# Rows of two degree tables: one-hot products on TensorE in place of 98 gathers

## The chip, the cores and the metric

The kernel runs on one core of a Trainium2 chip. The metric is the device time of one execution in microseconds (us). Times are given as the median of several runs; the profile comes from one further execution.

## The reference

The model is a two-layer graph network on 6250 nodes with 256 features and 100,000 edges. Each layer adds a graph part, a mixing part and a feed-forward part with experts to `x`. The change concerns the graph part of the second layer:

```python
in_deg = jnp.minimum(segment_sum(ones, dst, num_nodes), MAX_IN_DEGREE - 1)    # MAX = 512
out_deg = jnp.minimum(segment_sum(ones, src, num_nodes), MAX_OUT_DEGREE - 1)
edge_proj = edge_attr @ W_sum + b_sum
sum3d = segment_sum(edge_proj, src, num_nodes)
cent_term = sigmoid(centralities @ W_cent + b_cent)
vor_term = sigmoid(voronoi_values @ W_vor + b_vor)
return x + z_in[in_deg] + z_out[out_deg] + cent_term + vor_term + sum3d
```

`z_in` and `z_out` are tables of 512 rows of 256 numbers. Every node takes one row of each, chosen by its in-degree and its out-degree.

## The kernel before

Nodes lie in 49 tiles of 128 (the last has 106), called NT; edges lie in 782 tiles of 128, called W1C. All numbers are f32.

**The stage around the change.** The function `middle` first chooses two experts for each node (`gating`), then runs, in this order, `experts`, `take_back` and `mix1`; the function `between` follows. `experts` runs 32 slots of 512 node rows, and each of the 4 steps of a slot has 2 halves: two 128x512 products (L1417) and a Gelu on ScalarE (L1419), and, for the slot before, four 128x256 products (L1425) and an addition on VectorE (L1427). Eight transposes (L1400) turn the next slot's rows. Weights (512 KB each), rows and biases come by SyncE's queue (SP), and so does the store of the results (L1433). `take_back` gathers two expert results for each node tile (98 gathers). `mix1` goes over the nodes twice, 13 groups of up to 4 tiles each, in 15 iterations.

**The work behind it.** Behind this foreground runs a chain of background work, written as Python generators: `edge_sums`, which is `edge_pass` (L620) over the 782 edge tiles, beside `others`: `gat_places` (49 row gathers) and then `node_terms`, the function of the change. For an edge tile, `edge_pass` gathers 128 rows by GpSimd (POOL; `gather`, L776), marks a one-hot matrix on VectorE (`mark`, L616), multiplies both on TensorE (L603) and, once every 4 tiles, adds the result on VectorE (L594). The rows go to a ring of 15 tiles, with the gather 11 tiles ahead of its product and the mark 8 ahead.

**What sets the order.** Each engine runs its instructions in the order in which the program writes them. That order is dealt out by hand: every generator yields the due cost of what it has just written, and the foreground calls `step(us)`, which advances the background until its due costs cover the call:

```python
def step(self, us):
    while self.behind is not None and us > self.ahead:
        cost = next(self.behind, None)
        ...
        self.ahead += cost
    self.ahead -= us

def beside(self, work, other, rate):
    due = 0.0
    for cost in work:
        yield cost
        due += rate * cost
        while other is not None and due > 0.0:
            cost = next(other, None)
            ...
```

`beside` lets `others` run with `edge_sums` at 0.7 units for each unit of edges; an edge tile yields 1.27 units. `experts` calls `step(3.8)` eight times a slot, `take_back` once `step(20.0)`, `mix1` 30 times `step(11.0)`. What is left of the background then is written out by `finish`.

**Node terms.** For each node tile, `node_terms` forms two tanh terms (L1519, L1520), gathers one row of each table for its 128 nodes (tiles `zg`, through L776), and for the tile before adds all up on VectorE (L1528 to L1533) and stores the sum to DRAM on SP (L1534, `terms`). `between` reads it later. It yields 30 + 2 units at first, then 1.0 + 2 x 1.27 a tile for making and 1.0 a tile for adding.

Other names: `BT` is a buffer of 128 x 12544 numbers in SBUF, of which `experts` uses the first 8192 columns; `mm()` takes the next of PSUM's banks of that name, 4 in this stage, used in turn; `node_column` writes a row of degrees to DRAM and turns it into a column for each node tile; `indeg` and `outdeg` are these columns.

Of the kernel before, what the change touches and what calls it, by code (L numbers as in the profile page):

```python
# [8 lines left out]
F32 = mybir.dt.float32  # L9
I32 = mybir.dt.int32  # L10
AF = mybir.ActivationFunctionType
OP = mybir.AluOpType
# [6 lines left out]
P = 128  # L19
N = 6250  # L20
NT = 49
NP = NT * P
LAST = N - (NT - 1) * P
C = 256
# [36 lines left out]
class Net:  # L61


    def __init__(self, ctx, tc, a, out):
        self.ctx, self.tc, self.nc, self.a, self.out = ctx, tc, tc.nc, a, out
        self.const = ctx.enter_context(tc.tile_pool(name="const", bufs=1))
        self.dram = ctx.enter_context(tc.tile_pool(name="dram", bufs=1, space=DRAM))
        self.scat = 0
        self.behind = None


# [623 lines left out]
    def node_column(self, row, name, dst):  # L695

        nc = self.nc
        flat = self.dram.tile([NT, P], F32, name=f"flat_{name}")
        nc.sync.dma_start(flat.rearrange("(o t) p -> o (t p)", o=1), row)
        with self.tc.tile_pool(name="column", bufs=1, side="right") as sp:  # L700
            tiles = sp.tile([NT, P], F32, name="tiles")
            nc.sync.dma_start(tiles, flat)
            pt = self.tr()
            nc.tensor.transpose(pt[:, 0:NT], tiles, self.ident[0:NT, 0:NT])
            nc.vector.tensor_copy(dst, pt[:, 0:NT])
# [784 lines left out]
    def node_terms(self, pool):  # L1490


        nc, a = self.nc, self.a
        self.terms = self.dram.tile([NP, C], F32, name="terms")
        bsum = self.vec(pool, "L1_gnn_b_sum")
        base = self.vec(pool, "L1_mix_b_out")
        parts = []
        for w, b, v in (("L1_gnn_W_cent", "L1_gnn_b_cent", "node_vec1_n2"),
                        ("L1_gnn_W_vor", "L1_gnn_b_vor", "node_vec1")):
            c = pool.tile([P, NT], F32, name=f"nv_{v}")  # L1500
            nc.vector.memset(c, 0.0)  # L1501
            with nc.allow_non_contiguous_dma(reason="one value a node"):
                nc.sync.dma_start(c[:, 0:NT - 1], a[v][0:(NT - 1) * P, :].rearrange("(t p) o -> p (t o)", p=P))
                nc.sync.dma_start(c[0:LAST, NT - 1:NT], a[v][(NT - 1) * P:N, :])
            parts.append((self.vec(pool, w), self.vec(pool, b), c))
        yield 30.0

        nc.vector.tensor_scalar(base, base, 1.0, None, op0=OP.add)
        idx = pool.tile([P, 2, NT], I32, name="zidx")
        nc.vector.tensor_scalar(idx[:, 0, :], self.indeg, 511.0, None, op0=OP.min)  # L1510
        nc.vector.tensor_scalar(idx[:, 1, :], self.outdeg, 511.0, None, op0=OP.min)
        yield 2.0
        begun = None
        for t in list(range(NT)) + [None]:
            if t is not None:
                s = [pool.tile([P, C], F32, name=f"sg{i}", bufs=2) for i in range(2)]
                z = [pool.tile([P, C], F32, name=f"zg{i}", bufs=2) for i in range(2)]
                for i, (w, b, c) in enumerate(parts):
                    nc.vector.scalar_tensor_tensor(s[i], w, c[:, t:t + 1], b, op0=OP.mult, op1=OP.add)  # L1519
                    nc.scalar.activation(s[i], s[i], AF.Tanh, scale=0.5)  # L1520
                    yield 0.5
                for i, name in enumerate(("L1_gnn_z_in", "L1_gnn_z_out")):
                    self.gather(z[i], a[name], idx[:, i, t:t + 1])
                    yield 1.27
            if begun is not None:
                t0, s0, z0 = begun
                x = s0[0]
                nc.vector.tensor_add(x, x, s0[1])  # L1528
                nc.vector.scalar_tensor_tensor(x, x, 0.5, z0[0], op0=OP.mult, op1=OP.add)
                nc.vector.tensor_add(x, x, z0[1])  # L1530
                yield 0.5
                nc.vector.tensor_add(x, x, base)
                nc.vector.scalar_tensor_tensor(x, bsum, self.outdeg[:, t0:t0 + 1], x, op0=OP.mult, op1=OP.add)  # L1533
                nc.sync.dma_start(self.terms[t0 * P:(t0 + 1) * P, :], x)  # L1534
                yield 0.5
            begun = None if t is None else (t, s, z)

    def middle(self, scales, sums):
        nc = self.nc
        self.sumsT = sums.tile([P, 1, NP], F32, name="sumsT")  # L1540
        nc.vector.memset(self.sumsT, 0.0)
        self.mixed = sums.tile([P, 2, C], F32, name="mixed")
        self.norms1 = self.norms(sums, "mix1")
        self.chosen = self.dram.tile([8 * CAP, C], F32, name="chosen")
        self.yielded = self.dram.tile([TAKEN * SLOT, C], F32, name="yielded")
        self.rows_out = 0
        with self.tc.tile_pool(name="takes", bufs=1) as tp:
            self.shares = tp.tile([P, 2, NT], F32, name="shares")
            self.pos = tp.tile([P, 2, NT], I32, name="pos")
            self.slot = tp.tile([1, 2, TAKEN], I32, name="slot_of")  # L1550
            with self.tc.tile_pool(name="biases", bufs=1) as bp:
                self.expert_biases(bp)
                self.gating(scales)
            with self.tc.tile_pool(name="edge", bufs=1, reuse_waits="tile") as edge:
                def others():
                    yield from self.alone(self.gat_places)
                    yield from self.alone(self.node_terms)
                self.after_this(self.beside(self.edge_sums(edge), others(), 0.7))
                with self.tc.tile_pool(name="ffn0", bufs=1, reuse_waits="tile") as pool:
                    self.experts(pool, 3.8)  # L1560
                    self.take_back(pool)
                with self.tc.tile_pool(name="mix1", bufs=1, reuse_waits="tile") as mp:
                    self.mix1(mp)
                with self.tc.manual_schedule():
                    self.finish()
        self.edge_pass_if(self.wide2, self.sumsT, None, self.a["edge_attr_128"], self.by_src,
                          EDGE_BITS, E1 - 1, None)

    def mix1(self, pool):


        nc, tc, a, BT = self.nc, self.tc, self.a, self.BT
# [16 lines left out]
        def at(i):  # L1589
            return quads[i] if 0 <= i < nq else None  # L1590
        nc.scalar.activation(sd, mv[:, :, 1], AF.Sqrt, bias=self.eps)
        self.invert(norms, 0, NT)
        with tc.manual_schedule():
            for i in range(nq + 2):
                if at(i):
                    t, n, _ = at(i)
                    for q in range(n):
                        x = self.xa[:, t + q, :]
                        nc.vector.tensor_scalar(x, x, mv[:, t + q, 0:1], r[:, t + q:t + q + 1],
                                                op0=OP.subtract, op1=OP.mult)  # L1600
                if at(i - 1):
                    t, n, _ = at(i - 1)
                    for j, pt in enumerate(self.turned(lambda q: self.xa[:, t + q, :], n)):
                        nc.scalar.copy(BT[:, j, t * P:(t + n) * P], pt)
                if at(i - 2):
                    t, n, m = at(i - 2)
                    k = n * P if m == P else m
                    pk = self.mm()
                    self.dense(pk[:, 0:n * P], w[:, :, P:2 * P], BT[:, :, t * P:(t + n) * P])
                    nc.vector.tensor_reduce(tops[:, i - 2:i - 1], pk[:, 0:k], axis=AX.X, op=OP.max)  # L1610
                    nc.scalar.copy(kT[:, t * P:t * P + n * P], pk[:, 0:n * P])
                self.step(11.0)
            top = pool.tile([P, 1], F32, name="top")
            nc.vector.tensor_reduce(top, tops, axis=AX.X, op=OP.max, negate=True)
            cx = self.mm("kv")
# [1 line left out]
            for i in range(nq + 2):  # L1617
                if at(i):
                    t, n, m = at(i)
# [3 lines left out]
                if at(i - 1):  # L1623
                    t, n, m = at(i - 1)
# [5 lines left out]
                if at(i - 2):  # L1630
                    t, n, m = at(i - 2)
                    ek = eks.pop(i - 2)
                    for q in range(n):
                        nc.tensor.matmul(cx[:, 0:C], lhsT=ek[:m, q, :], rhs=self.xa[:m, t + q, :],
                                         start=(t + q == 0), stop=(t + q == NT - 1))
                self.step(11.0)
        total = pool.tile([P, 1], F32, name="total")
        nc.vector.tensor_reduce(total, parts, axis=AX.X, op=OP.add)
        nc.vector.reciprocal(total, total)
# [509 lines left out]
```

## Time and profile before

| | |
|---|---|
| median of 3 runs | 5470.35 us (5465.84 to 5480.0) |
| the profiled execution | 5465.94 us, span 5464.2 us |
| PE busy (TensorE matmul) | 3804.3 us, 70% of the span |
| POOL busy (GpSimd) | 3682.1 us, 67% |
| DVE busy (VectorE) | 2738.3 us, 50% |
| ACT busy (ScalarE) | 1239.7 us, 23% |
| gathers of edge attributes | 782, mean 959 ns |
| gathers of table rows (`zg`) | 98, first at 3012.0 us, last at 3453.1 us |
| take-back gathers | 98, first at 3577.1 us, last at 3710.6 us |
| mean granted clock of TensorE | 0.753 |

PE is TensorE's matmuls, PEld its weight loads, DVE VectorE, ACT ScalarE, POOL GpSimd, SP SyncE with its DMA queue. A group of instructions is named by line, engine, operation, written and read tiles and shape; behind it stand its busy time, the mean of one in ns, and the idle time of its engine just before, with what ended it. "Issue" is idle time in which the engine waited for nothing that the profile shows. The granted clock is the share of TensorE's full clock.

### The profile page before, as it was taken

What the parts mean: (1) busy time and instruction counts of PE and PEld (TensorE: products, weight loads), DVE (VectorE), ACT (ScalarE), POOL (GpSimd) and SP (SyncE); (2) the same over time, 40 slices, a digit from 0 to 9 for tenths busy, and PEclk for the clock granted to TensorE, in tenths of its full rate; (3) what the DMA queues carried; (4) which work ended last, traced back from release to release, by engine and by line L of the source; (5) the groups of instructions that cost most, each with busy time, mean ns of one, the idle gap of its engine ahead of it and who ended that gap; (6) DMA issues with size and microseconds to landing.
All of it is one profiled execution on the core that took longest, in us unless ns stands there. A gap on an engine that the chain in (4) does not pass through costs nothing. (4 is left out here: it accounts for less than half of the span.)

```text
span 5464.2 us, 56784 instructions
## 1 busy us (share of the span) xinstructions
PE 3804.3 (70%) x16292; PEld 2792.4 (51%) x16292; DVE 2738.3 (50%) x7767; ACT 1239.7 (23%) x2840; POOL 3682.1 (67%) x4400
## 2 busy tenths in 40 slices
PE   5898989997677777884476788705676975875400
PEld 4666666664556666654354555503555653543300
DVE  6886655535887666437453555345334212212217
ACT  4994333335000000015111222101002211111100
POOL 1767777770777777742574777777754888888861
PEclk8778576668896566675698999957667997987755
DMA  5334333331333333332377555432224222222234
GB/s 189 116 96 135 88 94 92 89 100 58 98 106 98 96 99 99 107 87 74 135 260 161 160 176 166 127 90 58 53 68 121 69 54 45 64 54 41 51 92 160
DMA packets 382785, 563.75 MB, mean 103 GB/s; under 512 B 124687, under 2 KB 270278, under 8 KB 382286
## 3 DMA queue, kind: packets, MB, share of 16 engines
q0 software_dynamic: 150864, 331.19, 22.4%
q1 hardware_dynamic: 207812, 209.55, 12.2%
q10 hardware_dynamic: 23756, 18.97, 1.1%
q8 instruction: 140, 2.29, 0.2%
q14 instruction: 213, 1.74, 0.1%
HBM read 446.11 MB, written 113.72 MB: 102 GB/s over the span
## 5 line engine op out<-in xcount | busy, mean ns | idle before, releaser
L603 PE MATMUL es<-hot,ring 128*128 128x128 f32 x7820 | 1897.9, 374 | 722.7 <-DVE sumsT L594 211.5
L776 POOL DMA_INDIRECT ring<-table,src_of x1564 | 1616.2, 1033 | 778.0 <-issue 226.8
L603 PEld LDWEIGHTS es<-hot,ring 128*128 128x128 f32 x7820 | 1436.2, 250 | 1131.4 <-issue 313.9
L776 POOL DMA_INDIRECT ring<-in_edge_attr,edge_of x782 | 749.7, 959 | 321.9 <-PE es L603 130.9
L776 POOL DMA_INDIRECT G<-gtab,glist x800 | 787.4, 984 | 189.9 <-issue 155.5
L2067 PE MATMUL mm<-lw,lhT 128*128 128x256 f32 x1568 | 380.4, 385 | 223.5 <-ACT lhT L2061 172.3
L640 ACT ACTIVATE ring<-ring,w_of 128x256 f32<-128x256 f32 x782 | 385.8, 507 | 519.6 <-DMA ring<-table,src_of 484.9
L2067 PEld LDWEIGHTS mm<-lw,lhT 128*128 128x128 f32 x1568 | 301.5, 193 | 350.1 <-ACT lhT L2061 175.8
L594 DVE TENSOR_TENSOR BT<-BT,es 128x256 f32 x392 | 163.9, 418 | 497.7 <-PE es L603 496.5
L2059 PE MATMUL mm<-lxt,lw 128*128 128x512 f32 (+1 forms) x832 | 380.7, 584 | 33.9 <-DVE ly L2069 31.5
L618 DVE TENSOR_SCALAR hot<-numbers,node_of,w_of 128x128 f32<-128x128 f32 x782 | 292.7, 401 | 59.5 <-PE es L603 58.8
L2069 DVE TENSOR_TENSOR ly<-mm,lb 128x256 f32<-128x256 f32 x196 | 81.1, 423 | 475.3 <-PE mm L2067 471.2
L1425 PE MATMUL mm<-mw,BT 128*128 128x256 f32 x1024 | 262.7, 403 | 39.6 <-DVE nv_node_vec_n L1501 22.0
L616 DVE TENSOR_SCALAR hot<-numbers,node_of 128x128 f32<-128x128 f32 x782 | 242.5, 337 | 64.2 <-PE es L603 63.6
L1417 PE MATMUL mm<-BT,mw 128*128 128x512 f32 x512 | 259.1, 631 | 6.1 <-ACT BT L1401 4.0
L616 DVE TENSOR_SCALAR hot<-numbers,from_of 128x128 f32<-128x128 f32 x782 | 241.7, 345 | 22.3 <-PE es L603 22.1
L2061 ACT ACTIVATE lhT<-mm,lb 128x512 f32<-128x512 f32 (+1 forms) x208 | 136.9, 664 | 465.6 <-PE mm L2059 465.2
L2059 PEld LDWEIGHTS mm<-lxt,lw 128*128 128x128 f32 x832 | 160.0, 198 | 143.7 <-issue 100.9
L1425 PEld LDWEIGHTS mm<-mw,BT 128*128 128x128 f32 x1024 | 197.1, 203 | 66.5 <-DVE nv_node_vec_n L1501 22.9
L1304 POOL DMA_INDIRECT chosen<-z,pos x98 | 99.0, 1011 | 178.4 <-DVE chosen L1227 133.6
L611 PE MATMUL es<-hot,ones 128*1 128x128 bf16 x782 | 189.2, 242 | 0.0
L1855 DVE TENSOR_TENSOR ge<-G,ad 128x320 f32<-128x320 f32 x10 | 9.5, 949 | 342.0 <-DMA G<-gtab,glist 341.9
(531 smaller groups left out, 4757.8 us busy)
## 6 DMA issues: line engine op xcount, KB each, us to landing
mw<-in_L_ffn_W SPq DMA_DIRECT2D x64, 512.0 KB
ring<-table,src_of POOLq DMA_INDIRECT x1564
ye<-ly SPq DMA_DIRECT2D x48, 512.0 KB
yes<-ye SPq DMA_DIRECT2D x48, 512.0 KB
xs<-chosen SPq DMA_DIRECT2D x32, 512.0 KB
yielded<-BT SPq DMA_DIRECT2D x32, 512.0 KB
G<-gtab,glist POOLq DMA_INDIRECT x800
ring<-in_edge_attr,edge_of POOLq DMA_INDIRECT x782
```

Source lines behind the costliest of these rows:

```text
L594: nc.vector.tensor_tensor(dst, dst, ps[:, 0:h * P].rearrange("p (j n) -> p j n", j=h), op=OP.add)
L603: nc.tensor.matmul(ps[:, j * P:(j + 1) * P], lhsT=rows[:, j * P:(j + 1) * P], rhs=hot, start=(first and j == 0), stop=(last and j == h - 1))
L611: self.nc.tensor.matmul(ps, lhsT=self.ones16[:, 0:1], rhs=half, start=False, stop=False)
L616: self.nc.vector.tensor_scalar(dst, self.numbers, node, None, op0=OP.is_equal)
L618: self.nc.vector.tensor_scalar(dst, self.numbers, node, w, op0=OP.is_equal, op1=OP.mult)
L640: nc.scalar.activation(r, r, AF.Copy, scale=w[:, i:i + 1])
L776: self.nc.gpsimd.indirect_dma_start(out=dst, out_offset=None, in_=table, in_offset=bass.IndirectOffsetOnAxis(ap=idx, axis=0))
L1417: nc.tensor.matmul(ph, lhsT=w1s[s][:, j, c * P:(c + 1) * P], rhs=xTs[s % 2][:, j, :], start=(j == 0), stop=(j == 1))
L1425: nc.tensor.matmul(po[:, :C], lhsT=hTs[(s - 1) % 2][:, i, c * P:(c + 1) * P], rhs=w[:, i, :], start=(i == 0), stop=(i == 3))
L2059: nc.tensor.matmul(ph[:, :n * P], lhsT=w1[:, e, j, c * P:(c + 1) * P], rhs=xt[:, j, :n * P], start=(j == 0), stop=(j == 1))
L2061: nc.scalar.activation(hT[:, c, :n * P], ph[:, :n * P], AF.Gelu, bias=b1[:, e, c:c + 1])
L2067: nc.tensor.matmul(po[:, :C], lhsT=h0[:, i, c * P:(c + 1) * P], rhs=w2[:, e0, i, :], start=(i == 0), stop=(i == 3))
```

## The change

The 98 gathers of table rows go. Both tables are loaded to the chip once, into columns of `BT` that `experts` leaves free, as 4 blocks of 128 rows each. For each node tile, two loads on SP bring its degrees as a row, repeated over the 128 partitions (`degrees`, one tile ahead); eight instructions on VectorE compare the row, capped at 511, with the row numbers of the 4 blocks of both tables and write one-hot matrices (`hot`, two buffers); eight products of 128x128 by 128x256 on TensorE add up both rows in one PSUM bank, and one addition on VectorE reads it there. One addition of the 2 for the gathered rows goes. The degree rows are those that `node_column` had written to DRAM.

In the due costs, the gathers' 2 x 1.27 go and 0.5 for the marks comes. The steps of the foreground change with it: `experts` 3.8 to 3.4, `mix1` 11.0 to 9.0.

```diff
-        flat = self.dram.tile([NT, P], F32, name=f"flat_{name}")
+        flat = self.flat[name] = self.dram.tile([NT, P], F32, name=f"flat_{name}")
...
-        idx = pool.tile([P, 2, NT], I32, name="zidx")
-        nc.vector.tensor_scalar(idx[:, 0, :], self.indeg, 511.0, None, op0=OP.min)
-        nc.vector.tensor_scalar(idx[:, 1, :], self.outdeg, 511.0, None, op0=OP.min)
+        which = pool.tile([P, 4], F32, name="zrow")
+        nc.vector.tensor_scalar(which, self.iota[:, 0:4], float(P), self.lane, op0=OP.mult, op1=OP.add)
+
+        spare = self.BT.rearrange("p j n -> p (j n)")[:, 8192:]
+        zs = []
+        for name in ("L1_gnn_z_in", "L1_gnn_z_out"):
+            z = spare[:, 4 * C * len(zs):4 * C * (len(zs) + 1)].rearrange("p (j c) -> p j c", j=4)
+            nc.sync.dma_start(z, a[name].rearrange("(j p) c -> p j c", p=P))
+            zs.append(z)
+
+        def degrees(t):
+            d = pool.tile([P, 2, P], F32, name="degrow", bufs=3)
+            for i in range(2):
+                flat = self.flat[str(i + 1)]
+                nc.sync.dma_start(d[:, i, :], bass.AP(tensor=flat.tensor, offset=flat.offset + t * P,
+                                                      ap=[[0, P], [1, P]]))
+            return d
+        near = degrees(0)
         yield 2.0
...
-                z = [pool.tile([P, C], F32, name=f"zg{i}", bufs=2) for i in range(2)]
+                deg, near = near, degrees(t + 1) if t + 1 < NT else None
+
+                hot = spare[:, 2048 + 1024 * (t % 2):3072 + 1024 * (t % 2)].rearrange("p (i j n) -> p i j n", i=2, j=4)
+                for i in range(2):
+                    for j in range(4):
+                        nc.vector.tensor_scalar(hot[:, i, j, :], deg[:, i, :], 511.0,
+                                                which[:, j:j + 1], op0=OP.min, op1=OP.is_equal)
+                yield 0.5
...
-                for i, name in enumerate(("L1_gnn_z_in", "L1_gnn_z_out")):
-                    self.gather(z[i], a[name], idx[:, i, t:t + 1])
-                    yield 1.27
             if begun is not None:
-                t0, s0, z0 = begun
+                t0, s0, h0 = begun
+                pz = self.mm()
+                for i in range(8):
+                    nc.tensor.matmul(pz[:, 0:C], lhsT=h0[:, i // 4, i % 4, :], rhs=zs[i // 4][:, i % 4, :],
+                                     start=(i == 0), stop=(i == 7))
                 x = s0[0]
                 nc.vector.tensor_add(x, x, s0[1])
-                nc.vector.scalar_tensor_tensor(x, x, 0.5, z0[0], op0=OP.mult, op1=OP.add)
-                nc.vector.tensor_add(x, x, z0[1])
                 yield 0.5
+                nc.vector.scalar_tensor_tensor(x, x, 0.5, pz[:, 0:C], op0=OP.mult, op1=OP.add)
                 nc.vector.tensor_add(x, x, base)
...
-                    self.experts(pool, 3.8)
+                    self.experts(pool, 3.4)
...
-                self.step(11.0)
+                self.step(9.0)
```

More of the change, by code (lines that the diff above doesn't have):

```diff
@@ L68, in __init__ @@
         self.scat = 0
+        self.flat = {}
         self.behind = None
@@ L1535, in node_terms @@
                 yield 0.5
-            begun = None if t is None else (t, s, z)
+            begun = None if t is None else (t, s, hot)
     def middle(self, scales, sums):
@@ L1635, in mix1 @@
                                          start=(t + q == 0), stop=(t + q == NT - 1))
-                self.step(11.0)
+                self.step(9.0)
         total = pool.tile([P, 1], F32, name="total")
```

## The prediction

> **What bounds the kernel now.** The changed lines run in one stage only, so I looked for that stage first. The page's chain of waits is no help: it reaches back to 4068 us, behind the stage. I located the stage by its tiles (expert weights from 2696 us, the first two gathers that the change removes at 3012 and 3016 us, the take-back gathers from 3577 us, the next stage from 4066 us) and asked for the busy time of each engine between these marks; columns are length, then busy time and instructions of PE, PEld, DVE, ACT, POOL, then granted clock, DMA share, GB/s.
>
> ```profile
> core 0: us, PE busy (x) PEld busy (x) DVE busy (x) ACT busy (x) POOL busy (x), PEclk, DMA share, GB/s
> 2690.00:3003.00 313.00, 219.71 (x912) 154.56 (x913) 142.50 (x442) 50.22 (x71) 177.43 (x188) 0.86 0.71 204
> 3003.00:3460.00 457.00, 360.00 (x1512) 254.67 (x1511) 247.57 (x735) 108.73 (x206) 348.54 (x356) 0.91 0.53 168
> 3460.00:3577.00 117.00, 86.52 (x367) 61.81 (x365) 35.37 (x128) 11.28 (x15) 88.46 (x94) 0.86 0.32 91
> 3577.00:4066.00 489.00, 238.57 (x881) 173.78 (x881) 207.88 (x640) 32.49 (x68) 359.36 (x378) 0.65 0.24 64
> ```
>
> Call the rows A, B, C, D. POOL issues 356 gathers in B's 457 us, one each 1.28 us; 94 in C's 117 us, 1.245 each; 378 in D's 489 us, 1.29 each. To see whether that is POOL's own pace, I asked for the groups of instructions in B (busy time and mean ns, then idle time before and its releasers):
>
> ```profile
> L776 POOL DMA_INDIRECT ring<-in_edge_attr,edge_of x258 | 253.7, 983 | 78.7 <-issue 40.9 <-PE es L603 13.7 <-DMA ring<-in_edge_attr,edge_of 13.7
> L776 POOL DMA_INDIRECT zg<-in_L_gnn_z_in,zidx x49 | 48.1, 981 | 15.0 <-issue 4.9 <-DMA ring<-in_edge_attr,edge_of 3.7 <-DVE sg L1532 1.8
> L1425 PE MATMUL mm<-mw,BT 128*128 128x256 f32 x571 | 145.8, 401 | 5.0 <-ACT BT L1419 3.8 <-DVE BT L1427 1.2
> L603 PE MATMUL es<-hot,ring 128*128 128x128 f32 x509 | 91.8, 295 | 86.0 <-DVE sumsT L594 46.9 <-issue 32.8 <-DMA ring<-in_edge_attr,edge_of 3.4
> L616 DVE TENSOR_SCALAR hot<-numbers,from_of 128x128 f32<-128x128 f32 x256 | 82.7, 345 | 0.0
> L1519 DVE SCALAR_TENSOR_TENSOR sg<-v_L_gnn_W_cent,nv_node_vec_n,v_L_gnn_b_cent 128x256 f32<-128x256 f32 x49 | 23.8, 486 | 131.2 <-DMA terms<-sg 131.2
> ```
>
> A gather is 0.95 to 0.98 us busy with 0.30 us before it, whatever is named as releaser: some 1.25 us, back to back. So B, C and D are bound by the count of gathers; PE is 79% busy in B and idles in front of L603. Only A has a real hole, one POOL wait of 47.5 us in it.
>
> What a dense PE does shows in the timeline of PE in B (start, length, instructions):
>
> ```profile
> 3213.78 0.60 PE L1400 MATMUL mm<-ident,xs 128*128 128x128 f32 x4
> 3214.22 1.88 PE L1417 MATMUL mm<-BT,mw 128*128 128x512 f32 x4
> 3215.94 0.61 PE L603 MATMUL es<-hot,ring 128*128 128x128 f32 x4
> 3216.39 1.89 PE L1425 MATMUL mm<-mw,BT 128*128 128x256 f32 x8
> 3218.11 0.61 PE L603 MATMUL es<-hot,ring 128*128 128x128 f32 x4
> ```
>
> The starts matter, not the 379 ns of one: eight 128x256 instructions take 1.72 us of PE, 0.216 each; four 128x512 take 1.72, 0.43 each; four 128x128 take 0.44, 0.11 each. And f32 products come as two instructions (L1425 is 512 calls in the code and 1024 in the trace; L1400's transposes come once). One expert slot is then 8 x 0.11 + 16 x 0.43 + 32 x 0.216 = 14.7 us of PE, an edge tile 0.22.
>
> **The change part by part.** *Pace.* The background work is dealt out by its due costs, so its place is arithmetic. Before, a slot hands out 8 x 3.8 = 30.4 units, after 8 x 3.4 = 27.2. A node tile cost 1.0 + 2 x 1.27 + 1.0 = 4.54 units and drew 4.54 / 0.7 = 6.49 units of edges (5.1 edge tiles) with it; now it costs 0.5 + 1.0 + 1.0 = 2.5 and draws 3.57 (2.8 edge tiles). Before: 49 x 11.03 / 30.4 = 17.8 slots with 250 + 98 = 348 gathers, beside the 356 of B. After: 49 x 6.07 / 27.2 = 10.9 slots with 138 gathers.
>
> *Part A*: the same 139 units of other work and 157 edge tiles with it; the gathers stay 206, the slots go from 10.9 to 12.2. The two 512 KB table loads come on SP behind the 30-unit step. PE has room outside the hole; I add 3 us: 316.
>
> *Part B*: POOL needs 138 x 1.25 = 173 us. PE needs 10.9 x 14.7 = 160, 138 x 0.22 = 30, and the new products: 8 calls x 2 instructions x 0.216 = 3.46 us a tile, 169 in all; together 360 us with no gap. PE becomes the last engine here by far. How near it comes to dense, the trace shows in a stretch of A where hardly a gather was due, and in the next stage:
>
> ```profile
> 2972.00:2991.70 19.70, 19.70 (x104) 15.05 (x103) 8.93 (x34) 4.20 (x6) 15.07 (x16) 1.00 0.52 164
> 4068.00:4165.00 97.00, 95.75 (x548) 85.95 (x549) 69.91 (x234) 40.40 (x83) 34.54 (x35) 0.96 0.39 122
> ```
>
> A slot of 23 edge tiles, 14.7 + 5.1 = 19.8 by my sum, took 19.7 us at clock 1.00. So the low bound is 360. DVE is second: 392 marks of 128x128, not in the trace as such; from SBUF with one per-lane scalar L941 takes 280 ns, from PSUM L616 345 and with two scalars L618 401: 110 to 157 us, I take 110 (same memories as L941). The rest of DVE in B is 133 us of node-term work (the rows of L1519, L1528, L1529, L1532, L1533), 45 for L616, 10 for L594, 18 for L1427. That is 316, up to 363. It hides under PE's 360, but in-order queues of 316 and 360 that wait for each other leak: the product's reader (in L1529's place) now waits for PE, and behind it on DVE stand edge marks (due 8 edge tiles ahead), the expert sums L1427 that free PSUM banks, and L594, for all of which PE waits in turn. In exchange, the eight marks (2.2 us) stand before L1519, where DVE waited 131.2 us for the store of the terms (2.8 a tile). I take 5% over dense, 378; the bounds are 360 and, with 363 plus 1.5 us a tile of mutual waits, 437.
>
> *The 98 row loads on SP* are issued a tile (7.7 us) before use, at 0.33 us like L1534, 34 us of SP, which in B spends most time waiting for DVE. They can be late only behind expert weights; the longest such wait of DVE in the row above was 9.3 us. Nothing, or 1.6 us for a few tiles; within the bound of 437. Behind them on SP stand the slot's weights and biases (ACT waits 101 us for these biases in B, 5.6 a slot).
>
> *Part C*: to the first take-back gather POOL has to issue, by the units, (876.4 - 261.8) / 1.27 = 484 edge tiles, 16 more in take-back's step and 49 others, 549 in all (before 486 + 16 + 49 + 98 = 649). When B ends, 157 + 49 + 138 = 344 are done and some 4 more, as POOL, no longer late, runs to the end of its ring of 15. Left: 201 x 1.25 = 251, where there were 117 us. This is where the faster pace gives the time back: gathers not asked for in B are all asked for later.
>
> *Part D*: 98 gathers and 298 edge tiles (before 296): the 9.0 in place of 11.0 only moves edges from the step calls to the end (69 in place of 20). 489 both; 0 to 10 more if mix1's PE, at clock 0.65 here, becomes late.
>
> Sum: 316 + 378 + 251 + 489 = 1434, before 313 + 457 + 117 + 489 = 1376: 58 us more. Against the profiled 5465.94 that is 5524; the three runs have a median of 5470.35, 4 us above it, so 5530.
>
> The Trainium skill, "TensorE: Matmul & The Clock Gate", section "Step-by-step: what each phase is for", has a matmul stream one column a cycle, at 2.4 GHz: by it I estimate the 392 x 256 columns at 42 us, B at 244 and the whole 76 us faster than before. The trace speaks otherwise: L1425's 0.43 us a call is four times that, and decides. Against the change stands "GPSIMD Engine Reference", section "Engine selection", which sends data-dependent indexing to GPSIMD's gather and gives no price. The trace's price is 1.25 us of POOL a gather against 1.73 of PE for its four products.
>
> **The rivals.** *Faster: POOL's relief counts in full.* 98 x 1.25 = 122 us of gathers go, POOL bounds most of the stage, and PE has idle time. It decides only if POOL can work off later edges while PE is on the products: whole-stage PE to 3577 is 32 x 14.7 + 500 x 0.22 + 169 = 749, with 5% and 20 us of start 806, against 887: 5390. Against it: B would need 378 / 1.25 = 302 gathers where 138 are due, a lead of 164 tiles, and the ring has 15. The sign turns from a lead of some 50 tiles on (58 / 1.25, and the 4 it has).
>
> *Slower still: DVE and the row loads set B.* If each tile waits for the row load or for PE with DVE idle, B goes to 437 or a little above: 5590. For it: DVE's 131 us of waits on a store in the same queues. Against: a load is issued a tile ahead.
>
> *No change*: PE in B at 320, which its own 360 excludes, or a shorter A hole; 5470.
>
> **How the numbers follow.** Main case 0.70, slower still 0.14, faster 0.11, no change 0.05. A change under 0.3%, 16 us, could not be told from none here. Slower 0.84, same 0.05, faster 0.11. The range must leave out at most 2 in 10: from a dense B with D as it was (5510) less 20 for a shorter hole in A, to B at 437 with D's 10: 5490 to 5595. The main case's own range, 5495 to 5560, has B between 360 and 400, and A and D within 15.
>
> **What would show it.** Right: between the first and the last product of the tables some 360 to 400 us with PE above 92% busy at clock near 1.0 and POOL below half; after it about 250 us to the first take-back gather with one gather each 1.25 us; D unchanged. Wrong: POOL still issuing each 1.25 us in B, products spaced under 0.2 us, or DVE idle for row loads in most tiles.

## Result and profile after

The changed kernel takes 5516.44 us (median of 4 runs, 5509.32 to 5521.55); the kernel before took 5473.91 in the 4 runs beside it. The ratio is 1.0078, 95% interval 1.0063 to 1.0092: 42 us slower. The forecast was 5530. The profiled execution took 5517.3 us with a span of 5515.4.

The windows of the kernel after, cut at the same marks as before (rows A, B, C, D; columns are length, busy time and instructions of PE, PEld, DVE, ACT and POOL, granted clock, DMA share, GB/s):

```profile
2690.00:3021.00 331.00, 242.31 (x999) 170.63 (x1000) 146.65 (x458) 56.84 (x81) 179.79 (x191) 0.85 0.72 204
3021.00:3379.00 358.00, 357.35 (x1658) 286.67 (x1657) 256.76 (x892) 81.66 (x162) 141.05 (x144) 1.00 0.43 131
3379.00:3634.00 255.00, 203.97 (x910) 149.54 (x908) 80.53 (x296) 35.52 (x49) 191.49 (x203) 0.90 0.41 123
3634.00:4125.00 491.00, 245.58 (x889) 175.79 (x889) 209.78 (x643) 32.04 (x68) 360.93 (x380) 0.63 0.24 65
```

The bound of B has moved. POOL is busy 141 of 358 us where it was busy 349 of 457, and PE 357.35 of 358 at full clock. C shows where the relief of POOL went: 203 gathers in 255 us, one each 1.25, where 94 took 117. B is 99 us shorter and C 138 longer. The four parts add up to 1435 us, before 1376: 59 more, and what lies after D is 8 us shorter in this profile though its code is the same.

Groups of instructions in B of the kernel after (busy time, mean of one in ns, then idle time before and its releasers):

```profile
L1549 PE MATMUL mm<-BT 128*128 128x256 f32 x784 | 177.3, 379 | 0.0
L777 POOL DMA_INDIRECT ring<-in_edge_attr,edge_of x144 | 141.1, 980 | 213.6 <-PE es L604 194.3 <-issue 16.8 <-PE mm L1549 2.4
L1426 PE MATMUL mm<-mw,BT 128*128 128x256 f32 x348 | 82.4, 379 | 0.0
L1538 DVE TENSOR_SCALAR BT<-degrow,zrow 128x128 f32<-128x128 f32 x384 | 80.1, 290 | 6.8 <-DMA degrow<-flat 6.8
...
L604 PE MATMUL es<-hot,ring 128*128 128x128 f32 x270 | 46.7, 274 | 0.0
...
L1542 DVE SCALAR_TENSOR_TENSOR sg<-v_L_gnn_W_cent,nv_node_vec_n,v_L_gnn_b_cent 128x256 f32<-128x256 f32 x49 | 23.6, 482 | 31.1 <-DMA terms<-sg 30.9
```

L1549 is the new product, L1538 the new mark. The three groups of PE shown have no idle time before them, and PE is idle for 0.65 us of the whole window. The wait has changed sides: POOL stands 194.3 us for L604, the product that frees a place of the edge ring. That PE is what POOL waits for would not make it the bound by itself; that it is also never idle does. DVE's wait for the store of the terms fell from 131.2 us (at L1519 before) to 30.9.

The timeline of PE in the same window (start, length, instructions):

```profile
3203.49 0.61 PE L604 MATMUL es<-hot,ring 128*128 128x128 f32 x4
3203.93 0.60 PE L1401 MATMUL mm<-ident,xs 128*128 128x128 f32 x4
3204.37 1.88 PE L1418 MATMUL mm<-BT,mw 128*128 128x512 f32 x4
3206.09 0.38 PE L604 MATMUL es<-hot,ring 128*128 128x128 f32 x2
3206.31 3.62 PE L1549 MATMUL mm<-BT 128*128 128x256 f32 x16
3209.76 1.89 PE L1426 MATMUL mm<-mw,BT 128*128 128x256 f32 x8
```

The 16 instructions of one node tile's products take 3209.76 - 3206.31 = 3.45 us, 0.216 each, as L1425 did before.

### The profile page after: what moved, and what is told of

The parts are those of the page before. It is cut to its first block, busy times and chain, and to the rows that moved or that the text cites. A ratio compares the mean times of both kernels' runs of the same rounds, so it can differ in the third digit from the quotient of the medians.

```text
span 5515.4 us, 58579 instructions
## 1 busy us (share of the span) xinstructions
PE 3952.2 (72%) x17076; PEld 2930.1 (53%) x17076; DVE 2799.6 (51%) x8109; ACT 1238.7 (22%) x2840; POOL 3580.2 (65%) x4302
## 5 line engine op out<-in xcount | busy, mean ns | idle before, releaser
L604 PE MATMUL es<-hot,ring 128*128 128x128 f32 x7820 | 1905.4, 375 | 634.1 <-DMA ring<-table,src_of 183.9
L604 PEld LDWEIGHTS es<-hot,ring 128*128 128x128 f32 x7820 | 1442.4, 250 | 1033.8 <-issue 267.7
L1420 ACT ACTIVATE BT<-mm,mb 128x512 f32<-128x512 f32 x128 | 86.5, 685 | 423.9 <-DMA mb<-bias 272.4
```

The lines of the kernel that those rows point to most:

```text
L604: nc.tensor.matmul(ps[:, j * P:(j + 1) * P], lhsT=rows[:, j * P:(j + 1) * P], rhs=hot, start=(first and j == 0), stop=(last and j == h - 1))
```

## Experiments

All times of parts come from one profiled execution each, cut at the same five events: first expert weight load, first node tile, store of the last node tile, first take-back gather, first load of the next stage. (Cut so, A is 6 us shorter than in the windows above and D 1 to 2 longer; for the kernel before, B is 3 shorter and C 2 longer.) Ratios are to the kernel before in the same session. The kernels `e2`, `e3`, `e9`, `e11` and `e13` add no rows of `z_out`, or wrong ones: they measure a part and are no versions to use.

| kernel | A | B | C | D | sum | ratio, 95% interval |
|---|---|---|---|---|---|---|
| before | 307 | 454 | 119 | 490 | 1371 | 1 |
| after | 325 | 358 | 255 | 493 | 1430 | 1.0078 [1.0063, 1.0092] |
| e1_old_pace | 314 | 342 | 353 | 406 | 1414 | 1.0059 [1.0043, 1.0076] |
| e5_before_new_pace | 315 | 455 | 18 | 592 | 1380 | 1.0027 [1.0017, 1.0038] |
| e3_half_marks | 320 | 360 | 254 | 492 | 1426 | 1.0071 [1.0048, 1.0093] |
| e2_half_products | 318 | 324 | 254 | 493 | 1389 | 1.0019 [1.0009, 1.0029] |
| e9_half_both | 315 | 319 | 254 | 493 | 1382 | 1.0013 [1.0002, 1.0024] |
| e11_early_biases | 318 | 324 | 254 | 492 | 1388 | 0.9999 [0.9988, 1.0009] |
| e13_four_sums | 311 | 277 | 253 | 491 | 1332 | 0.9932 [0.9909, 0.9954] |
| e8_before_spread_pace | 290 | 451 | 469 | 208 | 1417 | 1.0087 [1.007, 1.0103] |
| e4_spread | 296 | 660 | 12 | 328 | 1297 | 0.9846 [0.9828, 0.9864] |
| e10_spread_pair | 296 | 613 | 21 | 328 | 1259 | 0.9794 [0.9777, 0.981] |
| e12_spread_pair_early | 285 | 615 | 21 | 328 | 1250 | 0.9758 [0.9741, 0.9774] |
| e14_spread_pair_four | 289 | 589 | 21 | 328 | 1227 | 0.9726 [0.9706, 0.9747] |

A, whose own work is the same in the kernels of one pace, varies by 14 us between profiles (311 to 325). So the 18 us that A of the kernel after has over before are not all the change's; with the new steps alone (`e5_before_new_pace`) A takes 315.

### The pace

Two edits: the changed kernel with the steps of before, and the kernel before with the new steps.

```diff
-                    self.experts(pool, 3.4)
+                    self.experts(pool, 3.8)
...
-                self.step(9.0)
+                self.step(11.0)
```

> The changed kernel with the foreground's steps back at 3.8 and 11.0; the one-hot products stay. Theory (the products make TensorE last while 49 node tiles are worked off, and the gathers not asked for there are asked for later): the tile phase stays bound by TensorE, 9.8 slots x 14.7 + 30 + 169 = 343 us against 358, and the gathers stay 929, so the total is within -10 to +45 us of the changed kernel (the upper end because the edges run out some 7 iterations before mix1 ends). Rival (the faster pace is what costs): back to the kernel before, some 45 us faster than the changed kernel, ratio to before 1.000 +- 0.003.

```diff
-                    self.experts(pool, 3.8)
+                    self.experts(pool, 3.4)
...
-                self.step(11.0)
+                self.step(9.0)
```

> The kernel before (98 gathers, no products) with the changed kernel's steps of 3.4 and 9.0. Theory: POOL issues back to back in nearly the whole stage, so the order of the foreground moves nothing: gathers 1027 as before, stage 1376 -8 to +10 us, ratio to before 0.998 to 1.003. Rival (the pace edits made a part of the 42 us): ratio 1.004 to 1.008.

With the old steps the changed kernel took 5499.26 us where before took 5466.34, 0.0019 or some 10 us less than with the new ones. B was 342 with PE busy 341.10, where the theory had 343, C 353 and D 406: the larger steps hand out more edges ahead of the take-back, so C is 98 us longer and D 87 shorter. Before with the new steps took 5471.12 where before took 5455.87. So of the ratio 1.0078 the new steps explain some 0.002 (1.0078 - 1.0059), with intervals that touch; the other 0.006 come with the products. That the pace alone costs the time is out.

### What sets B: products or marks

`e2_half_products` leaves out the four products of `z_out` a tile; `e3_half_marks` leaves out the marks and row loads of the out-degree and multiplies the in-degree's marks with both tables.

```diff
-                for i in range(8):
+                for i in range(4):
                     nc.tensor.matmul(pz[:, 0:C], lhsT=h0[:, i // 4, i % 4, :], rhs=zs[i // 4][:, i % 4, :],
-                                     start=(i == 0), stop=(i == 7))
+                                     start=(i == 0), stop=(i == 3))
```

> The changed kernel with the four products of the second table left out (the z_out rows are not added); marks, row loads and due costs stay. Theory: 49 x 4 x 0.43 = 85 us less of TensorE in the tile phase, which shrinks from 358 to about 275 us, and the whole by 75 to 85 us, to below the kernel before: ratio to before 0.992 to 0.995. Rival (the marks and waits of VectorE or the row loads set the phase): it shrinks by less than 25 us, ratio above 1.003.

```diff
-                flat = self.flat[str(i + 1)]          # in degrees(), for i in range(2)
+                flat = self.flat[str(i + 1)]          # for i in range(1)
...
-                for i in range(2):
+                for i in range(1):
                     for j in range(4):
                         nc.vector.tensor_scalar(hot[:, i, j, :], deg[:, i, :], 511.0,
...
-                    nc.tensor.matmul(pz[:, 0:C], lhsT=h0[:, i // 4, i % 4, :], rhs=zs[i // 4][:, i % 4, :],
+                    nc.tensor.matmul(pz[:, 0:C], lhsT=h0[:, 0, i % 4, :], rhs=zs[i // 4][:, i % 4, :],
```

> The changed kernel with the marks and the row load of the out-degrees left out: both tables' products use the in-degree's one-hot matrices, so VectorE has 196 marks less (57 us) and SP 49 loads less, TensorE the same. Theory: no change, -8 to +8 us against the changed kernel, ratio to before 1.006 to 1.010, tile phase 350 to 362 us. Rival (VectorE or the row loads set the phase): 30 to 55 us less, ratio to before below 1.003.

The windows B of `e3_half_marks` and then of `e2_half_products`:

```profile
3007.00:3367.00 360.00, 359.61 (x1668) 288.36 (x1666) 220.52 (x699) 82.33 (x163) 140.37 (x146) 1.00 0.40 122
3007.00:3331.00 324.00, 291.60 (x1279) 221.33 (x1278) 254.58 (x893) 79.31 (x163) 141.82 (x145) 0.96 0.48 144
```

Half the marks less: DVE's busy time fell from 257 to 221 us, B took 360 and the ratio was 1.0071. Halving the marks and row loads changes nothing while PE is dense. Half the products less: B fell from 358 to 324, not to the 275 that PE's sum allows, and the ratio of 1.0019 lies between what the theory and the rival expected. PE is not dense here: 32 us idle, and a clock of 0.96. So there is a second bound at some 320 us under the first. Three guesses were tried at it.

### The second bound: two guesses that fell, one that held

`e9_half_both` takes VectorE's load away as well: both edits above together, so that the whole `z_out` table is left out (its products, marks and row loads).

> The changed kernel without the second table at all: its four products, its four marks and its row load of each node tile are left out (the z_out rows are not added). With the products alone left out the tile phase came to 324 us, not 275: VectorE had 255 us of work and some 60 us of waits there. Theory (a second bound, VectorE's queue, lies at 320 us under TensorE's 358): now TensorE has 275 us and VectorE 255 - 57 = 198 us and waits, so the tile phase falls to 275 to 300 us, 60 to 80 us under the changed kernel's, ratio to before 0.993 to 0.998. Rival (the 324 us were set by something else, the weights' and biases' loads or PSUM banks): it stays at 315 to 325 us, ratio 1.001 to 1.004.

Its window B, and the wait for the bias tile `mb` there (engine and line, what it waited for, us in total, times, longest):

```profile
3016.00:3335.00 319.00, 290.20 (x1275) 220.10 (x1274) 217.35 (x700) 79.89 (x164) 143.87 (x146) 0.97 0.45 137
ACT BT L1420 <- DMA mb<-bias: 70.6, 11, 9.6
```

B stayed at 319 us with DVE busy only 217, so VectorE's load is not the second bound. PE paused in most slots, 1 to 5 us after ScalarE's Gelu had waited for its bias. `e11_early_biases` therefore loads the biases a slot earlier:

```diff
         def first(s):
             if s < TAKEN:
                 w = w1s[s] = pool.tile([P, 2, 512], F32, name="mw1", bufs=2)
...
+                b = bs[s] = [pool.tile([P, n], F32, name=f"mb{i}", bufs=3) for i, n in ((1, 4), (2, C))]
+                for t, v in zip(b, (self.bias1, self.bias2)):
+                    nc.sync.dma_start(t, v[bass.ds(r, 1)].rearrange("e p n -> (e p) n"))
...
-                w2s[s] = w, b
+                w2s[s] = w, bs.pop(s)
```

> Leaves out the whole z_out table (its products, marks and row loads), as e9_half_both does; in addition the two bias tiles of a slot are loaded with its first weight, at the start of the slot before, and no longer behind the store at that slot's end. Nothing else differs from e9_half_both, whose tile phase took 319 us with PE busy 290.20, eleven PE pauses and 70.6 us of ScalarE waits for the bias tile. Theory (the bias load at the end of a slot sets the second bound): the pauses go, the waits of the line L1420 for mb fall below 20 us in the phase, the phase takes 285 to 300 us; the 20 to 30 us saved are partly given back in the phase after it, which is bound by gathers (POOL issued 141 in the phase; with less time under it the gathers before the end stay the same number), so the ratio to the kernel before falls by no more than 0.006 from 1.0013, to 0.995 to 1.001. Rival one (the banks or VectorE's queue set it, the bias is only named last): the phase stays at 310 to 325 us with pauses of another name, ratio 1.000 to 1.003. Rival two (a gain that is not given back): the phase at 290 us and the following parts unchanged, ratio 0.994 to 0.997.

The waits for `mb` are gone, all of them, and B is no shorter (324). So the late bias is not what holds B at 320 by itself. What does shows in this kernel's list of waits in B:

```profile
POOL ring L777 <- PE es L604: 160.0, 86, 8.8
DVE sg L1543 <- DMA terms<-sg: 76.1, 44, 6.4
PE mm L1550 <- DVE BT L1429: 9.5, 4, 3.1
```

and in three timelines of one such pause, SP's queue first:

```profile
3097.37 0.32 SPq L1558 DMA_DIRECT2D terms<-sg  x1
...
3098.23 0.46 SPq L1435 DMA_DIRECT2D yielded<-BT  x1
3099.20 0.39 SPq L1395 DMA_DIRECT2D mw<-in_L_ffn_W  x1
3100.58 0.34 SPq L1380 DMA_DIRECT2D xs<-chosen  x1
3101.43 0.38 SPq L1386 DMA_DIRECT2D mw<-in_L_ffn_W  x1
...
3103.34 0.59 SPq L1558 DMA_DIRECT2D terms<-sg  x1
```

then VectorE:

```profile
3103.43 0.34 DVE L617 TENSOR_SCALAR hot<-numbers,from_of 128x128 f32<-128x128 f32 x1
3109.08 0.48 DVE L1543 SCALAR_TENSOR_TENSOR sg<-v_L_gnn_W_cent,nv_node_vec_n,v_L_gnn_b_cent 128x256 f32<-128x256 f32 x1 [5.30 <-DMA terms<-sg]
3109.48 0.48 DVE L1543 SCALAR_TENSOR_TENSOR sg<-v_L_gnn_W_vor,nv_node_vec,v_L_gnn_b_vor 128x256 f32<-128x256 f32 x1
...
3110.47 0.42 DVE L1429 TENSOR_TENSOR BT<-mm,mb 128x256 f32<-128x256 f32 x1
```

and PE:

```profile
3107.54 0.38 PE L604 MATMUL es<-hot,ring 128*128 128x128 f32 x2
3110.94 1.99 PE L1550 MATMUL mm<-BT 128*128 128x256 f32 x8 [3.01 <-DVE BT L1429]
```

Read from the top: the store of a node tile's sum (128 KB, L1558) is issued at 3103.34, behind four transfers of 512 KB each (results, both weights, rows) and the biases (130 KB). VectorE's next node tile needs the buffer that this store empties, of which there are two, and stands 5.30 us until 3109.08. Behind it in VectorE's queue stands L1429, which reads the expert sums out of a PSUM bank; it comes at 3110.47, and PE, which needs a bank for the next products, stands 3.01 us. The store just before, issued at 3097.37 ahead of the large ones, was waited for only 0.77 us, until 3099.16. It is so all through B: 8 of the 44 waits follow a store behind the four large transfers, 4.1 to 6.4 us each and 42 of the 76 us together; the other 36 are at most 2.6 us, most of them under 0.9. Of PE's 30 idle us the list names L1429 for 12; for others it names ScalarE or nothing. The page "DMA: Bandwidth & Descriptors" of the Trainium skill, section "Queues, rings and completion order", says that each DMA engine takes the descriptors of one issuing queue in the order of its ring; the long landing behind the four large transfers agrees with that. No run moves the store to another queue, so whether the order of the queue or the load on the DMA engines makes it late is open.

`e13_four_sums` gives that tile four buffers:

```diff
-                s = [pool.tile([P, C], F32, name=f"sg{i}", bufs=2) for i in range(2)]
+                s = [pool.tile([P, C], F32, name=f"sg{i}", bufs=4 - 2 * i) for i in range(2)]
```

> e11_early_biases (the z_out table left out) with four buffers in place of two for the tile sg0 that holds a node tile's sum until its store has landed; nothing else differs. In e11_early_biases the tile phase took 324 us with PE busy 293.59; VectorE waited 76.1 us in 44 pieces for the store of the sum (terms<-sg), 5 to 6 us at a time when a slot's two 512 KB weight loads were under way, and PE paused 3 us behind it, in front of products that waited for the expert sums. Theory (the store's landing is the second bound of the phase): VectorE's wait for the store falls below 10 us, the pauses of PE named by the expert sums' line go, the phase takes 290 to 303 us, ratio to the kernel before 0.994 to 0.997 (e11_early_biases had 0.9999). Rival (another wait steps in its place, the weights or the edge ring): the phase stays at 310 to 325, ratio 0.998 to 1.002.

Its window B:

```profile
2997.00:3274.00 277.00, 275.90 (x1284) 214.81 (x1283) 216.33 (x699) 81.81 (x163) 141.22 (x147) 1.00 0.51 158
```

B is 47 us shorter, more than expected; PE is dense again, at full clock, the wait for `terms<-sg` is absent from the list, and PE's waits for L1429 have fallen to 1.0 us. The result is close to what PE's sum asks for: 358 - 392 x 0.216 = 273. The gain is kept, as C and D did not grow: 5424.19 us, ratio 0.9932 where `e11_early_biases` had 0.9999. With the biases early, the second bound is the wait for a store's landing with two buffers; that it lands late because of the large transfers ahead of it rests on the timeline. Four buffers without the early biases were not tried, so whether the late biases would hold B by themselves is open.

### The order of the work

The forecast's rival "faster" asked that POOL work off later edges while PE is on the products. `e4_spread` makes room for that without touching an instruction: a node tile asks 6 units more, so that more edge tiles and expert work lie between two tiles, and the steps are set so that the node tiles reach to the take-back.

```diff
                 nc.vector.tensor_add(x, x, s0[1])
-                yield 0.5
+                yield 6.5
...
-                    self.experts(pool, 3.4)
+                    self.experts(pool, 5.2)
...
-                self.step(9.0)
+                self.step(6.0)
```

> The changed kernel with other due costs only: a node tile yields 6.0 more units, experts steps 5.2, mix1 6.0; every instruction is the same, only their order differs, so that about two node tiles fall on a slot from slot 8 to the last. Theory (POOL's 122 us are given back only because the tiles come in a bunch and the ring lets it run 15 tiles ahead): per slot TensorE 14.7 + 2 x 3.46 + 4.3 = 25.8 us and POOL 19.5 x 1.25 = 24.4, so both stay busy; first take-back gather after 678 gathers x 1.25 + 70 us of hole and start, some 920 us after the stage begins, then 249 gathers x 1.28 = 320: stage 1240 to 1300 against 1376 before and 1435 changed, ratio to before 0.975 to 0.988. Rival (the products or their waits cost by themselves wherever they stand): not under the kernel before, ratio 1.000 or more.

Its windows B and C:

```profile
2985.00:3645.00 660.00, 636.01 (x3058) 499.95 (x3056) 381.02 (x1361) 134.48 (x237) 453.59 (x470) 0.98 0.47 143
3645.00:3657.00 12.00, 2.85 (x12) 1.61 (x10) 2.25 (x9) 0.00 (x0) 9.10 (x10) 0.66 0.40 111
```

The same 17076 matmuls and 4302 POOL instructions as in the kernel after, 5380.75 us. By the ratios that is 0.0232 less than the kernel after, some 127 us, and 1.5% faster than before. B and C together were 613 us with 347 gathers; now they are 672 with 480, and D falls from 493 to 328, as its gathers are done. PE is busy 636 of 660 us and POOL at the same time 454: the two loads lie over each other instead of after each other. The ratio is as the theory had it, but not by its parts: the first take-back gather came 968 us after the stage began, not 920, as PE and not POOL is the last engine in this B.

Could the kernel before have had this from the steps alone? `e8_before_spread_pace` gives it the steps of 5.2 and 6.0, not the 6 units a node tile.

> The kernel before with the steps of the spread kernel, 5.2 and 6.0. Theory: bound by the same 1027 gathers, so ratio to before 0.993 to 1.003; the gain of the spread kernel (ratio 0.985) comes from the 98 gathers it does not issue. Rival (the gain of the spread kernel is one of pace alone, which the gathers would give too): ratio 0.980 to 0.988.

No: with 5.2 and 6.0 it took 5497.52 us, outside what either theory expected. Its windows from the first take-back gather on:

```profile
3893.00:4030.00 137.00, 4.76 (x23) 4.79 (x24) 81.13 (x213) 1.51 (x3) 93.69 (x98) 0.50 0.33 94
4030.00:4100.00 70.00, 62.25 (x300) 44.82 (x298) 32.91 (x76) 28.98 (x65) 0.00 (x0) 0.98 0.01 3
```

All edge gathers were issued by 3891.5 us. So nothing was left to run behind the take-back and `mix1`, and the 70 us of `mix1`, hidden behind gathers before, now stand alone with POOL at 0. Its node tiles still come in a bunch (B 451 us), so it is not the order of `e4_spread`; the kernel before with its node tiles spread as well was not tried. An estimate: the rows before have 188 + 356 + 94 + 378 = 1016 gathers in the stage, 1270 us at 1.25, and with A's hole of 47.5 us some 1318 us, 53 under its 1371 but still above the 1297 of `e4_spread`.

### Cheaper products on top of the new order

`e10_spread_pair` keeps the order of `e4_spread` and splits each table into two bf16 tables (the rounded value and what remains), with bf16 marks: 16 products of bf16 a tile in place of 8 of f32.

```diff
+        z = spare[:, 0:2048]
+        zp = spare[:, 2048:4096].bitcast(BF16).rearrange("p (h n) -> p h n", h=2)
+        nc.vector.tensor_copy(zp[:, 0, :], z)
+        nc.vector.tensor_sub(zp[:, 1, :], z, zp[:, 0, :])
...
-                for i in range(8):
-                    nc.tensor.matmul(pz[:, 0:C], lhsT=h0[:, i // 4, i % 4, :], rhs=zs[i // 4][:, i % 4, :],
-                                     start=(i == 0), stop=(i == 7))
+                for i in range(16):
+                    nc.tensor.matmul(pz[:, 0:C], lhsT=h0[:, i // 8, i // 2 % 4, :],
+                                     rhs=zp[:, i % 2, i // 2 * C:(i // 2 + 1) * C],
+                                     start=(i == 0), stop=(i == 15))
```

> The spread kernel with each table held as two bf16 tables, the rounded value and the rest, and bf16 one-hot matrices: 16 bf16 products of 128x256 a node tile in place of 8 f32 ones; pace and order as in the spread kernel. Theory (in the spread kernel's tile phase of 660 us TensorE was busy 636 and POOL 454, so TensorE is still last there): if a bf16 product is one instruction of 0.108 us, a tile costs 1.73 us in place of 3.46, TensorE 85 us less; then POOL's 470 x 1.25 = 588 is last, phase 590 to 615, the whole 45 to 70 us under the spread kernel, ratio to before 0.972 to 0.977. Rival (the spread kernel's phase is set by VectorE or by loads): unchanged, ratio 0.982 to 0.987.

The group of its products in B, and one node tile's products in the timeline of PE:

```profile
L1553 PE MATMUL mm<-BT 128*128 128x256 bf16 x784 | 93.6, 273 | 0.0
...
3104.17 1.91 PE L1553 MATMUL mm<-BT 128*128 128x256 bf16 x16
3105.92 0.60 PE L1401 MATMUL mm<-ident,xs 128*128 128x128 f32 x4
```

Sixteen bf16 instructions take 3105.92 - 3104.17 = 1.75 us, 0.109 each, where the f32 products of a tile took 3.45. That is 84 us of PE less (177.3 to 93.6), and B 47 shorter (613): the stretch was as expected, the ratio 0.9794 a little worse than the 0.972 to 0.977 asked for. PE was idle 49 us in B, in the first half mostly once a slot. At that time the late biases still passed for the cause:

> e10_spread_pair with the two bias tiles of a slot loaded with its first weight, at the start of the slot before; nothing else differs. In e10_spread_pair the stretch from the first marks to the take-back took 613 us with PE busy 564.48 and clock 0.96. Theory (the pauses of PE in that stretch, once a slot, come from the late biases): PE's idle time there falls from 49 us to 20 to 30, the stretch to 580 to 600 us, and since the gathers are spread over it the gain is kept but for 5 us: ratio 0.9735 to 0.978 where e10_spread_pair had 0.9794. Rival (POOL's 461 gathers and the waits of the edge ring set it): stretch 605 to 620, ratio 0.978 to 0.981.

The ratio 0.9758 fell into the theory's range, but the theory fell: B stayed at 615. The ratio is lower all the same, by 0.0036 or some 20 us, with intervals that do not touch. In the profiles, A is 11 us shorter: there ScalarE waited 128.2 us for biases in `e10_spread_pair` and not at all here. So the early biases seem to pay in A and not in B; how much of it is A's own variation is open. VectorE waited 72.0 us for `terms<-sg` in B, much as in `e11_early_biases`. So the buffers again, with the same edit as in `e13_four_sums`:

> e12_spread_pair_early with four buffers in place of two for sg0; nothing else differs. There the stretch from the first marks to the last sum took 616 us with PE busy 568.29, POOL issued 464 gathers in it, and VectorE waited 72.0 us for the store of the sum. Theory: the waits for the store fall below 10 us and the stretch to 585 to 600 us, where POOL's 464 gathers at 1.25 us (580 us) become the bound: ratio 0.970 to 0.974, where e12_spread_pair_early had 0.9758. Rival (VectorE's waits for the store are covered by PE and POOL here): stretch 608 to 620, ratio 0.975 to 0.977.

Its windows B and C:

```profile
2988.00:3577.00 589.00, 558.01 (x3047) 423.90 (x3045) 380.15 (x1362) 137.65 (x237) 448.10 (x463) 0.99 0.52 159
3577.00:3598.00 21.00, 7.82 (x23) 5.25 (x22) 2.12 (x8) 0.00 (x0) 15.87 (x17) 0.51 0.32 84
```

Two waits in this B:

```profile
POOL ring L777 <- issue: 70.7, 232, 0.3
PE es L604 <- DMA ring<-in_edge_attr,edge_of: 29.1, 39, 1.8
```

B took 589, as expected, and no wait for `terms<-sg` is left: 463 gathers at 1.25 are 579, POOL issues them with 0.3 us between two, and PE, busy 558, waits for gathered rows. So POOL is the bound again. At 5315.64 us, ratio 0.9726 (0.9706 to 0.9747), this is the fastest version: 147 us under the kernel before.

## Why the prediction was right

**The main case held.** PE took POOL's place as the bound of B, and the gathers not issued there came back in C at 1.25 us each. The stage's sum came out at 1435 against 1434, but its terms erred by +15 (A), -20 (B), +4 (C) and +2 (D): that they cancelled is luck.

**B was mis-sized by the leak.** 360 dense plus 5% was 378; measured 358, PE busy 357.35. Dense PE was right to 2 us. The 18 us of leak were wrong. They rested on DVE at 316 us as nearly a second bound; DVE was busy 257. The marks were taken at 280 ns each, 110 us; one does take 290 ns, but eight in a row overlap, and 384 of them were busy 80.1 us, 0.209 each. The other half of the error is that the rows of DVE were added up: in the kernel after they add up to 288 us where DVE was busy 257, and in the kernel before to 285 where the prediction's own window has 248, as instructions of different rows overlap too. The timelines had been read so for PE (starts, not lengths) and not for DVE: in the lines above, L1543's 0.48 us is more than the 0.40 from one start to the next. `e3_half_marks` shows that at 257 us DVE's load costs nothing; what 316 would have cost no run shows.

**A** was forecast at 316 and took 331 in that profile. In other kernels with the same A (`e2_half_products`, `e3_half_marks`, `e13_four_sums`) it lay 5 to 14 us lower, so a good part of the miss belongs to the one profile. The rest is the 3 us that the prediction added for the new pace, which were too few: `e5_before_new_pace`, with the new steps alone, has A 8 us longer than before. With an A of 316 the stage's sum is 50 us above before; the ratio says 43 for the whole (0.0078 x 5474).

**C and D** were 255 and 491 against 251 and 489. D's 298 edge tiles (before 296) count the 16 of take-back's step twice: D has 380 gathers, before 378. Nothing came of it, as D's time was taken from the row before. The upper end of the range is 5599 by its own terms (5530 + 59 + 10), not 5595. **The row loads** cost 6.8 us of DVE's waits, hidden, as forecast.

**Slower still** fell: B at 437 asked for mutual waits of 1.5 us a tile, and PE had none. Its suspicion that VectorE's wait for the store of the terms matters was good in another place: once half of the products are out and the biases early, that wait sets B (`e13_four_sums`), and the forecast's list of bounds (PE, POOL, DVE's load) did not hold it. That is the likely reason why half of the products less gave 34 us and not 85.

**Faster** fell for the kernel as written, by the reason given: POOL's lead ends with the ring, and it stood 194.3 us for the product that frees a place there. With the tiles spread over the stage the sign turned, to 5380.75 where the rival had said 5390. That the totals agree is in part luck: the rival had 806 us to the first take-back gather and D unchanged at 489, measured were 968 and 328. A deeper ring in place of the new order, with the lead of some 50 tiles that the prediction named, was not tried.

**The price of an f32 product** is what makes PE the last engine in B. A call of 128x256 costs 0.43 us in f32 and 0.109 in bf16, from start to start. The page "TensorE: Matmul & The Clock Gate" of the Trainium skill, cited in the prediction for one column a cycle, fits the bf16 row: 256 columns at 2.4 GHz are an estimated 0.107. For f32 another of its pages, "FP8 and Floating Point Precision", section "TensorE Precision Notes", has the rule: true f32 takes four passes through the array. The rows agree, 0.43 / 0.109 = 3.9.

## What to carry to other kernels

Moving work from a loaded engine to an idle one pays only if both can run at the same time: where work is dealt out in a fixed order, look how far the relieved engine can run ahead before it stands for the loaded one, and spread the moved work until that lead suffices. A wait that ends just before a pause need not be its cause: taking the late bias away alone left B as long as it was, and only the run that took the wait for the store away as well shortened it. When a cut gives less than its size, the next bound has been reached; here it was a buffer that waits for its store, in a row that looked harmless while another engine covered it.

## What the runs showed of the hardware

A 128 KB store issued behind four transfers of 512 KB on SP's queue held its buffer for 5.7 us (3103.34 to 3109.08); the one issued ahead of them held it for 1.8 us (3097.37 to 3099.16). A bf16 product of 128x256 took 0.109 us from start to start, an f32 call 0.43. In B, marks written as bf16 were no cheaper than as f32: 81.9 us for 390 of them in `e10_spread_pair` against 80.1 for 384 in the kernel after. The granted clock of TensorE in B was 1.00 where PE was busy 357 of 358 us and 276 of 277, and 0.95 where it was busy 294 of 324.
